# Forming the first attention scores earlier, and adding the last block's attention in halves from an earlier tile, in a fused attention and mixture-of-experts kernel

## The chip, the cores and the metric

The kernel runs on one core of a Trainium2 chip. The metric is the device time of one execution in microseconds (us), lower is better; the number quoted is the median of several runs. A core has five engines that run side by side and wait for each other through semaphores: PE (TensorE, matrix multiplies and transposes), DVE (VectorE), ACT (ScalarE), POOL (GpSimd, which here mostly issues gathers and adding stores) and SP (SyncE, which here only issues DMA).

## What is computed

The input is x of shape (8, 1024, 256). Its rows are layer-normalised, then two results are added to x: causal linear attention of 16 heads, and a mixture of 8 experts of which each row uses two. Cut to what matters:

```python
xn = layernorm(x)
q = elu(xn @ Wq.T) + 1; k = elu(xn @ Wk.T) + 1; v = xn @ Wv.T      # 16 heads of 16
kv_cumsum = cumsum(k_outer_v, axis=1); k_cumsum = cumsum(k, axis=1)
att = (q . kv_cumsum) / clip(q . k_cumsum, 1e-6) @ Wo.T
w, e = top_k(xn @ Wr + br, 2); w = softmax(w)
moe = sum over both e of w_e * (silu(xn @ W1[e]) * (xn @ W3[e])) @ W2[e]
out = x + att + moe
```

All data are float32.

## The kernel before, in words

The 8192 rows form 16 blocks of 512 (two per sequence). The experts' work is not done by blocks but by tiles: rows that chose the same expert are listed, and tiles of 128 listed rows are gathered from x in device memory, multiplied with that expert's weights and added back to the output by an indirect store. There are 135 tiles, of which the last three run only if they hold rows, so the main loop has NM = 132 tiles.

*The start* (lines 1047 to 1118) is written in a fixed order for DVE, ACT, PE and POOL. The first four blocks are normalised, turned and routed (`moments`, `normalise`, `turn`, `logits`, `route`), and `first_batch` makes from them the list of the first 25 tiles. Beside it block 0's q, k and v are projected. At its end stand the row statistics of block 5 (`moments(FB + 1, 1)`, DVE), three steps of block 0's attention (`attend_upto(3, False)`: transposes of k, L858, and on DVE the running sums of k, L863 to L868), two matmuls whose result nobody reads (`idle_ps`, L1113), and a switch of ACT to the Silu table (L1118). Meanwhile POOL gathers the rows of tile 0 (`ffn_load`, L1162 the rows, L1167 their weights and norm numbers).

*The main loop* (line 1285) does for tile j: `ffn_step` (load tile j + 3, weights of tile j + 2 through SP, the hidden products gu_ps L1216, the turning of tile j + 1's rows xg_t L1183, the output y_ps L1235 of tile j - 1, and its adding store L1246 on POOL). In the first tiles it also normalises, turns and routes the remaining blocks, and it calls `attend_upto`, which advances the attention. Outside the part with a fixed order a scheduler places the instructions on each engine.

*The attention* is a generator of 9 steps per block, 144 in all (`block_steps`, line 995). Steps 1 to 4 project q, k, v and form the denominators (den, L880; over, L886; they go through device memory by den_d and return as rden, L892 and L898); step 5 forms the scores of the block's first 128 rows (`scores`: s_ps, L919, in four banks of the pool ps_mm; the mask s_sb on DVE, L926; the state kv_ps L934 and kv L939); steps 6 to 9 weigh (`weigh`: o_ps, L953 and L960, oT) and multiply with Wo (`attend`: a_ps L979, ACT's copy into at L984). A block's four quarters of at are added to the output by one POOL DMA at its end (L989); only the last block adds each quarter by itself (L987). How far the attention is at tile j comes from a formula in the loop: slow up to tile 21, and from tile 22 on evenly (L1325), so that the last step runs at tile 127.

*What orders writes of the output.* Adding DMAs to the same array wait for the one before to land, and POOL issues them one after another.

Of the kernel before, what the change touches and what calls it, by code (L numbers as in the profile page):

```python
# [53 lines left out]
P = 128  # L54
# [9 lines left out]
def tile_attention_moe(  # L64
# [208 lines left out]
    def moments(t, n):  # L273


        def small(name, *shape, dtype=F32):
            return f_two.tile([P, n * NCH, *shape], dtype, tag=name, name=name)

        less, rstd = (tab[:, t * NCH : (t + n) * NCH, w] for w in (1, 2))
        st = small("st", 6)  # L280
        mv = small("mv", 2)
        for c in range(n * NCH):
            nc.vector.bn_stats(st[:, c, :], xbs[t + c // NCH][:, c % NCH, :])
            nc.vector.bn_aggr(mv[:, c, :], st[:, c, :])
        v = small("v")
        nc.vector.tensor_scalar(v, mv[:, :, 1], EPS_NORM, None, ALU.add)
        if t <= FB:
            nc.gpsimd.tensor_tensor(rstd, v, neg_half, ALU.pow)
        else:

            half = small("half")
            nc.vector.tensor_scalar(half, v, -0.5, None, ALU.mult)
            bits = small("bits", dtype=I32)
            nc.vector.tensor_scalar(bits, v.bitcast(I32), 1, None, ALU.arith_shift_right)
            nc.vector.tensor_scalar(bits, bits, -1.0, float(0x5F3759DF), ALU.mult, ALU.add)
            y = bits.bitcast(F32)
            for i in range(4):
                sq = small("sq")
                nc.vector.tensor_tensor(sq, y, y, ALU.mult)
                nc.vector.tensor_tensor(sq, sq, half, ALU.mult)  # L300
                y_new = small(f"y{i % 2}") if i < 3 else rstd
                nc.vector.scalar_tensor_tensor(y_new, sq, 1.5, y, ALU.add, ALU.mult)
                y = y_new
        yield
        nc.vector.scalar_tensor_tensor(less, mv[:, :, 0], -1.0, rstd, ALU.mult, ALU.mult)
        yield
# [665 lines left out]
    def attend(t, c, oT):  # L972


        if c == 0:
            ats[t] = one.tile([P, NCH, H], F32, tag="at", name=f"at{t}")
        a_ps = ps_y.tile([P, H], F32, tag="y", name="a_ps")
        for hh in range(2):
            nc.tensor.matmul(  # L979
                a_ps, lhsT=oT[:, hh, :], rhs=wo_sb[:, hh, :],  # L980
                start=(hh == 0), stop=(hh == 1),
            )
        at = ats[t]
        nc.scalar.copy(at[:, c, :], a_ps)  # L984
        to = acc_f if t < FB and not copied else of
        if t == NBLK - 1:
            nc.gpsimd.dma_start(out=to[t][:, c, :], in_=at[:, c, :], accum_op=ALU.add)  # L987
        elif c == NCH - 1:
            nc.gpsimd.dma_start(out=to[t], in_=at, accum_op=ALU.add)  # L989
        if c == NCH - 1:  # L990
            del ats[t], blocks[t]
# [3 lines left out]
    def block_steps(t):  # L995


        for i, _ in enumerate(project(t)):
            if i == 1 and behind:
                attend(*behind.pop())  # L1000
            if i in (1, 3, 5, 8):
                yield
        if t + 1 < NBLK:
            fetch(t + 1)
        waiting = scores(t, 0)
        yield
        done = None
        for c in range(NCH):
            coming = scores(t, c + 1) if c + 1 < NCH else None
            if done and c + 1 < NCH:  # L1010
                attend(*done)
            oT = weigh(*waiting)
            if done and c + 1 == NCH:
                attend(*done)
            done = t, c, oT
            waiting = coming
            if c + 1 < NCH or t + 1 < NBLK:
                yield
        behind.append(done)
        if t + 1 == NBLK:  # L1020
            attend(*behind.pop())
            yield
# [24 lines left out]
    with tc.manual_schedule(engines={EN.DVE, EN.Activation, EN.PE, EN.Pool}):  # L1047
        parts = [moments(t, 1) for t in range(FB)]
        lgT4 = e_one.tile([P, FB, P], F32, name="lgT4")
        small_constants()  # L1050
        next(parts[0])
        qs = [project_q(0, o) for o in range(KC)]
        for t in range(FB):
            if t + 1 < FB:
                next(parts[t + 1])
            next(parts[t])
            normalise(t)
            turn(t)
            if t == 1:
                logits(0, lgT4[:, 0, :])  # L1060
            elif t == 0:
                xnTs[0] = turned_first.pop()
                begin(0)
            if t < KC:
                next(qs[t])
        last_moments = moments(FB, 1)
        next(last_moments)
        for t in range(1, FB):
            logits(t, lgT4[:, t, :])
        for _ in last_moments:  # L1070
            pass
        lg4 = ps_t.tile([P, FB * P], F32, tag="t", name="lg4")
        for t in range(FB):
            nc.tensor.transpose(lg4[:, bass.ts(t, P)], lgT4[:, t, :], ident)
        store(FB - 1)
        add_logits(0, FB, lg4)
        for q in qs:
            next(q)
        normalise(FB)
        ks = [project_k(0, c) for c in range(0, NCH, 2)]  # L1080
        routing = route(0, FB)
        next(routing)
        next(ks[0])
        next(routing)
        turn(FB)
        next(ks[1])
        for q in qs:
            next(q)
        next(routing)
        listing = first_batch()  # L1090
        next(listing)
        next(routing)
        lg_t = logits_turned(FB)
        vs = [project_v(0, c) for c in range(0, NCH, 2)]
        next(vs[0])
        next(listing)
        next(vs[0])
        next(listing)
        add_logits(FB, 1, lg_t)
        next(listing)  # L1100
        for o in range(KC):
            mask_q(0, o)
        next(vs[1])
        for k in ks:
            next(k)
        for _ in moments(FB + 1, 1):
            pass
        next(vs[1])
        attend_upto(3, False)

        for _ in range(2):
            idle_ps = ps_mm.tile([P, TB], F32, tag="mm", name="idle_ps")
            nc.tensor.matmul(  # L1113
                idle_ps, lhsT=ident, rhs=blocks[0][0][:, 0, :], start=True, stop=True
            )
        next(routing)

        nc.scalar.activation(warm, ones[:, 0:1], AF.Silu)  # L1118
# [166 lines left out]
    for j in range(NM + 1):  # L1285
        if j + 1 < NM:
            ffn_norm(j + 1)
        t = FB + j
        if FB < t <= NBLK and t % ROUND == 0:
            for _ in routing:  # L1290
                pass
        if 0 < j and t < NBLK:
            if j % 2 == 0:
                with tc.issue_after(last_token[0].ins):
                    for _ in moments(t, 2):
                        pass
            normalise(t)
            turn(t)
            if t + 5 < NBLK:
                load_x(t + 5, nc.scalar)  # L1300
            add_logits(t, 1, logits_turned(t))
            if (t + 1) % ROUND == 0:
                routing = route(t + 1 - ROUND, t + 1)
                next(routing)
        if j == LISTS:
            in_order(
                nc.sync.dma_start(
                    out=tab_d[1][1 : 1 + NS * P, :].rearrange("(p i) w -> p (i w)", p=P),
                    in_=tab.rearrange("p i w -> p (i w)"),
                )  # L1310
            )
            in_order(nc.sync.dma_start(out=tab_d[1][0:1, :], in_=before[0:1, 0:3]))
            lists = second_batch(taken)
        if LISTS <= j < READ:
            next(lists)
        if LISTS <= j < LISTS + NBLK - FB:
            t = FB + j - LISTS
            rows = slice(t * TB, (t + 1) * TB)
            in_order(nc.sync.dma_start(out=out_rows[rows, :], in_=x_rows[rows, :]))
        if j < LISTS:  # L1320
            attend_upto(3 + j // 2)
        elif j < READ:
            attend_upto(AHEAD - 3 * (READ - j - 1) // 2)
        else:
            attend_upto(AHEAD + (NBLK * STEPS - AHEAD) * (j - READ + 1) // (NM - READ - 4))  # L1325
        if j == N1 + 1:
            copied.append(j)
            in_order(nc.sync.dma_start(out=out_rows[0 : FT * P, :], in_=acc_d[:, :]))
        ffn_step(j, LATE if N1 < j <= N1 + LATE else 0)
# [54 lines left out]
```

## Time and profile before

| | us |
|---|---|
| median of 3 runs | 1318.28 (1317.63 to 1319.15) |
| the profiled execution's own time | 1329.68 |
| its span, first to last instruction | 1328.0 |
| PE busy in the span | 1270.6 |
| DVE, ACT, POOL busy | 636.9, 526.1, 523.1 |
| last matmul of the gu_ps group ends | 1314.6 |

The profile is of one execution. A busy share is an average over stages; what a stage is bound by is read from the stretch itself: which engine is full there, and which wait ends last. In a timeline line the first number is the start in us from the span's start, the second the duration, and the bracket gives the idle time of that engine just before and what ended it. A matmul of float32 leaves two records, so "x32" are 16 matmuls. "PEclk" is the share of the full clock that PE was granted.

### The profile page before, as it was taken

To read this page: it belongs to the slowest core of one execution; us is meant where nothing else is said; L and a number is where in the kernel's file an instruction comes from. 1 tells how busy PE (TensorE), PEld (TensorE's weight loads), DVE (VectorE), ACT (ScalarE), POOL (GpSimd) and SP (SyncE) were. 2 spreads that over 40 slices of the span, in tenths; PEclk is the share of its full clock that TensorE was granted. 3 is DMA by queue.
4 is the path that set the end of the run, shared out by engine and by line. 5 is a ranking of instruction groups with operands and counts; after the bars stand their busy time and mean duration, and the time that the engine had idled before them with its cause. 6 is when DMAs were issued, how large, how long until landed. Compare 5 with 4: busy or idle time off the path is not lost.

```text
span 1328.0 us, 28290 instructions
## 1 busy us (share of the span) xinstructions
PE 1270.6 (96%) x10968; PEld 1092.2 (82%) x10968; DVE 636.9 (48%) x1436; ACT 526.1 (40%) x1060; POOL 523.1 (39%) x460
## 2 busy tenths in 40 slices
PE   5689999999999999999999999999999999999996
PEld 4478887787888888888888888898888888888886
DVE  7667489764252434435343535344443525243441
ACT  4466364461524325161525243341515152433411
POOL 3633333233254443443443525343434334343432
PEclk9899999999999999999999999999999999999998
DMA  9688576466685766666675757476676767575763
GB/s 340 229 276 258 154 200 170 130 173 206 176 229 141 198 166 155 189 173 172 169 190 145 216 132 208 126 188 171 160 186 170 189 153 194 147 198 134 198 161 72
DMA packets 163462, 240.36 MB, mean 181 GB/s; under 512 B 16098, under 2 KB 87394, under 8 KB 163042
## 3 DMA queue, kind: packets, MB, share of 16 engines
q1 hardware_dynamic: 119938, 184.31, 45.0%
q0 software_dynamic: 38064, 43.22, 19.3%
q10 hardware_dynamic: 5328, 11.01, 2.3%
q8 instruction: 90, 1.47, 0.5%
q14 instruction: 42, 0.34, 0.1%
HBM read 196.30 MB, written 52.67 MB: 187 GB/s over the span
## 4 chain that ended last, share of the span: by engine, by line
PE 87%; DVE 7%; ACT 2%; issue 1%; DMA 1%; another core or an unknown queue 1%; POOL 0%; POOLq 0%; DVEq 0%; ACTq 0%
PE gu_ps L1216 34%; PE y_ps L1235 16%; PE o_ps L960 5%; PE s_ps L919 5%; PE a_ps L979 4%; PE zq L795 4%; PE zkk L811 4%; PE zkv L811 4%; PE kv_ps L934 2%; PE o_ps L953 2%; PE xg_t L1183 2%; DVE s_sb L926 1%; PE tp L333 1%; PE den L880 1%; PE tp L858 1%
## 5 line engine op out<-in xcount | busy, mean ns | idle before, releaser
L1216 PE MATMUL gu_ps<-xgT,w 128*128 128x128 f32 x4224 | 511.2, 278 | 8.9 <-DVE s_sb L926 7.6
L1216 PEld LDWEIGHTS gu_ps<-xgT,w 128*128 128x128 f32 x4224 | 492.5, 193 | 28.8 <-issue 12.5
L1162 POOL DMA_INDIRECT xg<-in_x_dram,src_i x132 | 128.1, 970 | 406.1 <-ACT xgT L1185 322.4
L1246 POOL DMA_INDIRECT out_dram<-y,dst_i x107 | 176.3, 1648 | 222.2 <-DVE kn L765 54.2
L1235 PE MATMUL y_ps<-w_sb,hT 128*128 x1056 | 250.6, 380 | 2.6 <-DVE hT L1227 2.0
L1227 DVE TENSOR_TENSOR hT<-gu_ps,hT 128x512 f32<-128x512 f32 x132 | 91.1, 690 | 274.4 <-PE gu_ps L1216 198.0
L1235 PEld LDWEIGHTS y_ps<-w_sb,hT 128*128 128x128 f32 x1056 | 190.2, 190 | 24.0 <-DVE hT L1227 1.9
L1224 ACT ACTIVATE hT<-gu_ps 128x512 f32<-128x512 f32 x132 | 78.8, 597 | 299.9 <-PE gu_ps L1216 255.0
L926 DVE TENSOR_TENSOR s_sb<-s_ps,causal 128x512 f32<-128x512 f32 x256 | 163.6, 684 | 54.0 <-PE s_ps L919 25.5
L1242 DVE TENSOR_SCALAR y<-y_ps,entry 128x256 f32<-128x256 f32 x132 | 63.5, 481 | 120.0 <-PE y_ps L1235 75.0
L1167 POOL DMA_INDIRECT entry<-tab_d,of_i x107 | 106.5, 995 | 32.6 <-issue 30.5
L1185 ACT COPY xgT<-xg_t 128x256 f32<-128x256 f32 x132 | 49.0, 371 | 145.2 <-PE xg_t L1183 141.7
L984 ACT COPY at<-a_ps 128x256 f32<-128x256 f32 x64 | 23.7, 370 | 159.2 <-PE a_ps L979 149.0
L919 PE MATMUL s_ps<-qm,kT 32*128 32x256 f32 x1024 | 85.5, 405 | 0.5 <-DVE hT L1227 0.4
L1174 ACT ACTIVATE xg<-xg,entry 128x256 f32<-128x256 f32 x132 | 79.6, 603 | 3.4 <-issue 3.4
L960 PE MATMUL o_ps<-s_sb,va 128*32 128x128 f32 x2048 | 73.2, 276 | 0.0
L919 PEld LDWEIGHTS s_ps<-qm,kT 32*128 32x128 f32 x1024 | 51.0, 184 | 24.2 <-issue 19.6
L979 PE MATMUL a_ps<-wo_sb,oT 128*128 128x256 f32 x256 | 69.0, 393 | 0.1
L1246 POOL DMA_INDIRECT acc_d<-y,src_i x25 | 44.0, 1761 | 55.2 <-DVE y L1242 15.4
L960 PEld LDWEIGHTS o_ps<-s_sb,va 128*32 128x32 f32 x2048 | 53.2, 109 | 9.8 <-DVE oT L967 0.8
L811 PE MATMUL zkk<-wkv_sb,xnT 128*128 128x256 f32 x256 | 60.0, 384 | 0.0
L795 PE MATMUL zq<-xnT,wq_sb 128*128 128x512 f32 x128 | 59.9, 609 | 0.0
(211 smaller groups left out, 1361.7 us busy)
## 6 DMA issues: line engine op xcount, KB each, us to landing
w<-in_w_dram SPq DMA_DIRECT2D x264, 512.0 KB
den_d<-over SPq DMA_DIRECT2D x64, 128.0 KB
rden<-den_d SPq DMA_DIRECT2D x16, 512.0 KB
xnT_d<-xnT ACTq DMA_DIRECT2D x15, 512.0 KB
xnT<-xnT_d SPq DMA_DIRECT2D x15, 512.0 KB
out_dram<-in_x_dram SPq DMA_DIRECT2D x12, 512.0 KB
out_dram<-at POOLq DMA_DIRECT2D x12, 512.0 KB
xb<-in_x_dram SPq DMA_DIRECT2D x10, 512.0 KB
```

What stands on the lines that cost most here:

```text
L795: nc.tensor.matmul(z, lhsT=wq_sb[:, k, bass.ts(o, P)], rhs=xnTs[t][:, k, :], start=(k == 0), stop=(k == KC - 1),)
L811: nc.tensor.matmul(z[:, i, :], lhsT=xnTs[t][:, k, bass.ts(c + i, P)], rhs=wkv_sb[:, k, a, :], start=(k == 0), stop=(k == KC - 1),)
L919: nc.tensor.matmul(s_ps[r][:, hh].rearrange("p a l -> p (a l)"), lhsT=kT[rows, hh, span], rhs=qm[rows, hh, :, span], start=True, stop=True,)
L926: nc.vector.tensor_tensor(sm, s_ps[r].rearrange("p k a l -> p (k a) l"), causal_b, ALU.mult)
L960: nc.tensor.matmul(o_ps[32 * r : 32 * r + 32, hh, :], lhsT=va[:, c, 4 * hh + r, a, :], rhs=s_sb[r][:, 2 * hh + a, :], start=(first and a = ...
L979: nc.tensor.matmul(a_ps, lhsT=oT[:, hh, :], rhs=wo_sb[:, hh, :], start=(hh == 0), stop=(hh == 1),)
L1162: nc.gpsimd.indirect_dma_start(out=xg[j], out_offset=None, in_=x_rows[:, :], in_offset=bass.IndirectOffsetOnAxis(ap=src_i[:, i : i + 1], a ...
L1167: nc.gpsimd.indirect_dma_start(out=entry[j], out_offset=None, in_=table[:, :], in_offset=bass.IndirectOffsetOnAxis(ap=num_i[:, i : i + 1], ...
L1216: done = nc.tensor.matmul(ps[:, i, :], lhsT=w13[:, k, bass.ts(i, P)], rhs=xgT[j][:, k, :], start=(k == 0), stop=(k == KC - 1),)
L1227: nc.vector.tensor_tensor(hT, gu[1], hT, ALU.mult)
L1235: done = nc.tensor.matmul(y_ps, lhsT=hT[:, i, :], rhs=w2_sb[:, bass.ds(e * (IC * H) + i * H, H)], start=(i == 0), stop=(i == IC - 1),)
L1246: nc.gpsimd.indirect_dma_start(out=rows[:, :], out_offset=bass.IndirectOffsetOnAxis(ap=dst_i[:, i : i + 1], axis=0), in_=ys.pop(j), in_off ...
```

## The change

Four edits:

- In block 0's attention the scores of the first 128 rows are formed after step 3, before the denominators (`if t == 0 and i == 5`); for other blocks nothing moves. Step 4 and step 5 of block 0 change places.
- In the start, `attend_upto(3, False)` is followed by `attend_upto(4)`, so those scores belong to the fixed order, and both stand ahead of the statistics of block 5. The idle matmuls are four in place of two and use one buffer of the pool ps_y, since the scores hold all four banks of ps_mm.
- The last block adds its attention in two halves of 256 columns by 128 rows by two, in place of four quarters.
- The formula of L1325 ends three tiles earlier (NM - READ - 7 in place of NM - READ - 4): the last attention step runs at tile 124.

```diff
         if t == NBLK - 1:
-            nc.gpsimd.dma_start(out=to[t][:, c, :], in_=at[:, c, :], accum_op=ALU.add)
+            if c % 2 == 1:
+                two_c = slice(c - 1, c + 1)
+                nc.gpsimd.dma_start(
+                    out=to[t][:, two_c, :], in_=at[:, two_c, :], accum_op=ALU.add
+                )
         elif c == NCH - 1:
...
             if i in (1, 3, 5, 8):
                 yield
+            if t == 0 and i == 5:
+                waiting = scores(t, 0)
+                yield
         if t + 1 < NBLK:
             fetch(t + 1)
-        waiting = scores(t, 0)
-        yield
+        if t > 0:
+            waiting = scores(t, 0)
+            yield
...
         for k in ks:
             next(k)
+        next(vs[1])
+        attend_upto(3, False)
+        attend_upto(4)
         for _ in moments(FB + 1, 1):
             pass
-        next(vs[1])
-        attend_upto(3, False)
-
-        for _ in range(2):
-            idle_ps = ps_mm.tile([P, TB], F32, tag="mm", name="idle_ps")
+
+        idle_ps = ps_y.tile([P, TB], F32, tag="y", name="idle_ps")
+        for _ in range(4):
             nc.tensor.matmul(
                 idle_ps, lhsT=ident, rhs=blocks[0][0][:, 0, :], start=True, stop=True
             )
...
-            attend_upto(AHEAD + (NBLK * STEPS - AHEAD) * (j - READ + 1) // (NM - READ - 4))
+            attend_upto(AHEAD + (NBLK * STEPS - AHEAD) * (j - READ + 1) // (NM - READ - 7))
```

## The prediction

> **What bounds the kernel now.** I read the page first: the busy shares and the chain that ended last.
>
> ```profile
> PE 1270.6 (96%) x10968; PEld 1092.2 (82%) x10968; DVE 636.9 (48%) x1436; ACT 526.1 (40%) x1060; POOL 523.1 (39%) x460
> ```
> ```profile
> PE 87%; DVE 7%; ACT 2%; issue 1%; DMA 1%; another core or an unknown queue 1%; POOL 0%; POOLq 0%; DVEq 0%; ACTq 0%
> ```
>
> TensorE (PE) is the bound, so an edit pays only where PE stands still. The view by stretches says where: from 400 to 1300 us PE is busy 99.5%; it is idle in the first 100 us and after the last matmul at 1314.6 us. The columns are PE, PEld, DVE, ACT and POOL busy us, granted clock, DMA share, GB/s:
>
> ```profile
> 40.00:50.00 10.00, 6.88 (x78) 4.42 (x70) 7.77 (x38) 5.82 (x12) 5.06 (x5) 1.00 1.02 344
> 50.00:60.00 10.00, 6.51 (x36) 5.88 (x36) 5.55 (x29) 1.47 (x3) 7.63 (x8) 0.66 0.27 76
> 60.00:70.00 10.00, 6.49 (x47) 5.66 (x48) 6.63 (x39) 5.16 (x11) 1.42 (x2) 0.83 0.43 138
> 90.00:100.00 10.00, 6.77 (x55) 5.37 (x54) 7.67 (x30) 5.61 (x9) 2.60 (x2) 1.00 1.07 321
> ```
>
> The timeline of PE, ACT and DVE then names the waits (start, duration, in brackets the idle time before and its releaser):
>
> ```profile
> 45.84 1.88 PE L1113 MATMUL idle_ps<-qT,ident 128*128 128x512 f32 x4
> 52.21 0.69 PE L1183 MATMUL xg_t<-ident,xg 128*128 128x128 f32 x2 [4.49 <-issue]
> 53.36 5.61 PE L1216 MATMUL gu_ps<-xgT,w 128*128 128x128 f32 x32 [0.46 <-issue]
> 63.49 0.33 PE L333 MATMUL tp<-ident,xb 128*128 128x128 f32 x1 [4.31 <-ACT xb L318]
> 91.67 1.15 PE L919 MATMUL s_ps<-qm,kT 32*128 32x256 f32 x16
> 96.22 2.27 PE L1216 MATMUL gu_ps<-xgT,w 128*128 128x128 f32 x18 [2.76 <-DVE s_sb L926]
> 98.97 0.49 PE L443 MATMUL cnt_ps<-both,upto_neg 128*128 128x128 f32 x2 [0.47 <-DVE both L429]
> ```
> ```profile
> 62.36 0.60 ACT L1224 ACTIVATE hT<-gu_ps 128x512 f32<-128x512 f32 x1 [8.55 <-remote]
> ```
>
> PE is idle 4.5 us while tile 0's rows come; then tile 0 runs 5.61 us where 32 such records take 3.57 us later (chain, 1292.69); PE waits 4.3 us for ACT, which had itself waited 8.55 us for something the trace does not show (gu_ps was finished by 58.97); and tile 0's scores, formed inside the PE-bound stretch, hold PE 2.76 us because DVE masks them late. At the end POOL's row-adding stores follow each other:
>
> ```profile
> 1293.50 1.61 POOL L1246 DMA_INDIRECT out_dram<-y,dst_i  x1 [4.51 <-DVE y L1242]
> 1299.96 1.56 POOL L1246 DMA_INDIRECT out_dram<-y,dst_i  x1 [4.85 <-DMA out_dram<-y,dst_i]
> 1306.28 1.55 POOL L1246 DMA_INDIRECT out_dram<-y,dst_i  x1 [4.76 <-DMA out_dram<-y,dst_i]
> 1310.82 1.55 POOL L1246 DMA_INDIRECT out_dram<-y,dst_i  x1 [3.00 <-issue]
> 1316.18 1.55 POOL L1246 DMA_INDIRECT out_dram<-y,dst_i  x1 [3.81 <-DVE hT L1227]
> 1320.84 1.55 POOL L1246 DMA_INDIRECT out_dram<-y,dst_i  x1 [3.11 <-DMA out_dram<-y,dst_i]
> ```
>
> The last y is ready at 1317.91 (DVE L1242), its store starts 2.93 us later, because the store ahead of it had not landed.
>
> **What the Trainium skill says.** "TensorE: Matmul & The Clock Gate", section "What's actually happening": after an idle window of about 3.4 us PE's clock falls to half, and about 3.4 us of work brings it back. The trace agrees: idle 47.72 to 52.21, clock 0.50 from 51 to 57 us. "DMA: Bandwidth & Descriptors", section "Two DMAs through the same engine are not ordered": a DMA that touches bytes of an earlier one must wait for its completion semaphore. The trace agrees: three of the six stores above were released by the previous store's DMA. Same page, section "Anatomy of one DMA — SWDGE (gpsimd) path": about 2.0 us fixed plus bytes/436e3, so as an estimate a 256 KB half costs 2.6 us and two 128 KB quarters 4.6 us one after the other; the trace has 4.2 to 5.3 us between POOL's last-block entries, neighbours included. Same page, "Issuing engines are not separate DMA queues": all share 16 engines; the stores above are 6.46 and 6.32 us apart while weights load (last issue 1300.03) and 4.54 to 5.36 after.
>
> **The change, part by part.** All sums stand against the profiled execution, 1329.68 us with a span of 1328.0; that is 11.4 us above the median 1318.28. The unexplained 8.55 us gap cost PE 4.3 us plus about 1.6 us of half clock (64 to 67.3), so it may be part of that excess. I work the start both without the gap (N) and with it (G).
>
> *Scores into the gather.* Removed from the stretch at 91.67: 8 s_ps and 2 kv_ps matmuls (1.7 us of PE, to 93.46), four s_sb and one kv on DVE (4 x 0.60 + 0.36). They now stand behind the k transposes: kT is ready at 46.68, so PE has them done near 48.4, inside the 4.5 us gap, cost nothing. Four idle matmuls at 0.94 (1.88 for two) then fill to 52.2, when xg_t can start; the clock should stay full and tile 0's gu takes 3.6 in place of 5.6. They use a ps_y buffer; if they overran, at most 0.5 us.
>
> *Statistics of block 5 moved behind the scores on DVE.* In the built order DVE now does, from 45.07 on: wait for kT to 46.2, two scans (1.20), two multiplies (0.6), four s_sb, kv: to about 52.8. Only then the statistics, which before took 45.0 to 54.2; with hT(0) (0.6) standing among them, tab is ready near 62.7. ACT's normalise (4 x 0.6), and PE's transposes of that block, queue behind it; PE has finished tiles 0 and 1's gu by 61.2 and waits. Behind those transposes stand the logits, xg_t(2), lg_t and y(0). Following ACT's order (normalise to 65.2, one more normalise at 66.1 that waits for the next statistics, two xnT copies to 67.7, two DMA issues 0.9, lgT) y(0) starts near 69.6.
> Before, in N: tab at 54.3, tp at 59, gu(1) beside it, y(0) near 66.0. So +3.6. In G: before 72.0; after, gu(1) starts at 63.4 behind the same gap, y(0) near 72.6: +0.6. Half clock after a thin stretch 61 to 69: 0 to 1.6, I take 0.8.
>
> *den moves two tiles later.* Its 8 matmuls (0.6), over (0.29 + 0.94), four den_d DMAs and rden pass two tiles of weight loads in SP's queue. From over to rden's issue it was 11.7 us (81.99 to 93.69); two tiles give some 20, so I take 0; up to 2 if oT waits for rden on DVE, with hT behind it. The fetch of xnT moves with it and is not wanted before tile 12.
>
> *Tile 4.* gu(4) no longer waits behind s_sb. Its counts (cnt_ps) still wait for DVE's routing, which starts after the xb DMA issued at 84.46 lands at 92.15. Without the 2.4 us of s_sb, "both" comes 4.3 us after that landing in place of 6.75; PE has by then done all 32 gu records, 14 more (1.55 us). Gain about 4.0 after paying den's 0.6; 2 to 5.5, as the xb DMA may land sooner without den_d beside it; I take 4.4.
>
> Start, N: 3.6 + 0.8 - 4.4 = 0.0. G: 0.6 - 4.4 = -3.8.
>
> *Middle.* 121 attention steps spread over 103 tiles, not 106: the same PE work, so 0; stalls by DVE there total some 14 us and move about, +-1.5.
>
> *End.* Last attend at tile 124 in place of 127; nothing on PE saved. POOL saves two issues of 0.9, hidden. But nine stores, not six, now follow each other at y's pace of 5.52 us (1292.73 to 1298.25), while a store under weight loads takes 6.3 to 6.5. The lag grew 0.29, 1.23, 2.03 in the old tail; three more tiles may add up to 0.85 each, less what the last quiet tiles give back. Bounds 0 and 3.0 (the lag can't shrink: the first of the six was on time); I take 1.2, since at a lag the store falls into other gaps of the weight traffic (one pair in mid-kernel was 5.52 apart).
>
> Sum N: 0.0 + 0 + 1.2: 1319.5 on the median.
>
> **Rivals.** *Faster:* the gap is real in every run, or ACT's queue is not held by the statistics; then the full clock, the avoided 2.76 and the 1.7 count. For it: the gap is in the trace. Against: 11.4 us of excess want an explanation. -3.8 and up to -1.6 for the second half-clock stretch, +1.2: 1314.3. *Slower:* the late statistics. Place: PE's first tp of block 5; price 3.6 plus 1.6 of half clock, with tile 4 giving back only 2; it decides as soon as PE is through gu(1) (61.2) before tab (62.7). With the tail at 2.5: 1324. For it: DVE is 1.00 busy from 45 to 53, so the pushed work has no slack. Against: ACT and DVE orders may let PE use that time. *Tail only:* start nets nothing and lag grows in full: 1321.3. That scores don't move is excluded: the built order shows them ahead of the idle matmuls.
>
> **How the numbers follow.** Forecast N 0.42 (its own range 1316.5 to 1322.5), faster 0.25, slower 0.25, tail only 0.08. A measurement of this kernel tells about 0.2% from no change, 2.6 us: bounds 1315.6 and 1320.9. From N one sixth lies above and little below; so faster 0.26, same 0.38, slower 0.36. Range 1313.5 to 1324.5.
>
> **What would show it.** Clock 1.0 and gu(0) near 3.6 us in 50 to 60; a PE wait at tp L333 near 61 to 65 with tab late (right for N and the slower rival; absent for the faster one); no wait at s_sb near 90; last store's start minus last y over 2.93 us. I am wrong if PE does not wait for block 5, or if the middle's stalls change by more than 2 us.

## The result, and the profile after

The changed kernel took 1323.23 us (median of 7 runs, 1322.84 to 1326.34) where the kernel before took 1319.84 (7 runs, 1317.63 to 1321.21). The ratio is 1.0034 with a 95% interval of 1.0022 to 1.0045: slower by a third of a per cent (the ratio weighs all runs; the medians alone lie 3.4 us apart). The profiled execution of the changed kernel has a span of 1321.2 us and an own time of 1323.23, so unlike the profile of before it is a typical one.

The page of the changed kernel, busy shares and chain:

```profile
PE 1273.1 (96%) x10972; PEld 1091.4 (83%) x10972; DVE 636.0 (48%) x1436; ACT 526.4 (40%) x1060; POOL 524.5 (40%) x458
PE 87%; DVE 8%; ACT 2%; DMA 2%; issue 1%; POOL 0%; POOLq 0%; ACTq 0%; DVEq 0%
```

The shares hardly differ from those before: a loss of 0.3% lies in a few waits. The stretches of the changed kernel (us, then busy us of PE, PEld, DVE, ACT, POOL, granted clock, DMA share, GB/s) show where the start was altered:

```profile
50.00:60.00 10.00, 8.53 (x61) 6.75 (x60) 10.00 (x47) 3.18 (x7) 7.56 (x9) 1.00 0.48 143
60.00:70.00 10.00, 6.66 (x44) 4.07 (x42) 8.05 (x58) 5.44 (x12) 3.17 (x4) 0.72 0.68 213
```

From 50 to 60 us PE is busy 8.53 us at full clock (6.51 at 0.66 before), and DVE is full. From 60 to 70 PE stands still as long as before and its clock has dropped. Below, gu(j) and y(j) are the hidden products and the output of tile j, and tab holds the scale and shift with which a block's rows are normalised. The timelines of PE and of ACT in the changed kernel name the waits:

```profile
48.17 3.60 PE L1122 MATMUL idle_ps<-qT,ident 128*128 128x512 f32 x8
...
53.22 3.84 PE L1225 MATMUL gu_ps<-xgT,w 128*128 128x128 f32 x32 [0.46 <-ACT xgT L1194]
...
63.82 0.33 PE L333 MATMUL tp<-ident,xb 128*128 128x128 f32 x1 [2.69 <-ACT xb L318]
...
70.46 3.75 PE L1244 MATMUL y_ps<-w_sb,hT 128*128 x8 [0.55 <-DVE lg_all L367]
...
116.32 1.16 PE L1225 MATMUL gu_ps<-xgT,w 128*128 128x128 f32 x8 [2.23 <-DVE s_sb L926]
```
```profile
63.17 2.08 ACT L318 ACTIVATE xb<-xb,tab 128x256 f32<-128x256 f32 x4 [2.74 <-DVE tab L305]
```

Tile 0's gu takes 3.84 us (5.61 before). Then PE waits 2.69 us for the normalised rows of block 5, for which ACT has waited for tab. y(0) runs at half clock. The wait of a gu for s_sb, 2.76 us at 96 us before, is gone from there, and one of 2.23 us stands at 116 us. ACT's gap of 8.55 us is not in this profile. The last stores on POOL:

```profile
1304.35 1.55 POOL L1255 DMA_INDIRECT out_dram<-y,dst_i  x1 [2.94 <-issue]
1309.62 1.55 POOL L1255 DMA_INDIRECT out_dram<-y,dst_i  x1 [3.72 <-issue]
1314.18 1.55 POOL L1255 DMA_INDIRECT out_dram<-y,dst_i  x1 [3.00 <-DMA out_dram<-y,dst_i]
```

The last y is ready at 1310.62, so its store starts 3.56 us later; before it was 2.93 us.

### The profile page after: what moved, and what is told of

Its sections match the earlier page's. It is cut to its first block, busy times and chain, and to the rows that moved or that the text cites. A ratio compares the mean times of both kernels' runs of the same rounds, so it can differ in the third digit from the quotient of the medians.

```text
span 1321.2 us, 28291 instructions
## 1 busy us (share of the span) xinstructions
PE 1273.1 (96%) x10972; PEld 1091.4 (83%) x10972; DVE 636.0 (48%) x1436; ACT 526.4 (40%) x1060; POOL 524.5 (40%) x458
## 4 chain that ended last, share of the span: by engine, by line
PE 87%; DVE 8%; ACT 2%; DMA 2%; issue 1%; POOL 0%; POOLq 0%; ACTq 0%; DVEq 0%
PE gu_ps L1225 34%; PE y_ps L1244 16%; PE s_ps L919 5%; PE o_ps L960 5%; PE a_ps L979 4%; PE zq L795 4%; PE zkk L811 4%; PE zkv L811 4%; PE kv_ps L934 2%; PE xg_t L1192 2%; PE o_ps L953 2%; DMA xb<-in_x_dram 1%; DVE st L283 1%; PE tp L858 1%; PE tp L333 1%
```

## The experiments

Each was timed beside the kernel before, in three comparisons on three chips. There the kernel before took 1327.4 to 1328.7 us, 8 to 9 us more than in the first comparison, whose chip is not on record. Whether the chip or the gap on ACT makes that difference was not separated. Ratios are to the kernel before of the same comparison.

**The kernel before once more, and the changed kernel once more** (no edit).

> The kernel before, unchanged, profiled a second time. Its first profile had a span of 1328.0 us, 8 us over its timed median, with a gap of 8.55 us on ACT in the start that nothing in the trace explains. If the gap was of that one execution, the new profile shows a span near 1317, no such gap, y(0) near 66 and the ratio is 1.000. If the gap belongs to the kernel, it is there again, y(0) is near 72, and the start of the changed kernel (y(0) at 70.5) gained instead of lost.

> The changed kernel, unchanged, beside the kernel before in the same call. If the start (1.0025 alone) and the end (1.0015 alone) simply add, the ratio is 1.004 (1.003 to 1.005). Its own first profile had no stall on ACT before 63 us; in the last call all four kernels had one, in which the semaphore of PE told of matmuls of 54 to 59 us only at 62.7. If that stall belongs to the program, it is here again and y(0) is near 78; if it depends on the chip, y(0) follows what before shows on the same chip.

Measured: 1.0000 (0.9991 to 1.0008) and 1.0032 (1.0017 to 1.0046), profiled spans 1326.2 and 1328.8. ACT's gap is in both. ACT in the kernel before, profiled again, and then in the changed kernel:

```profile
62.75 0.60 ACT L1224 ACTIVATE hT<-gu_ps 128x512 f32<-128x512 f32 x1 [8.37 <-remote]
```
```profile
63.02 0.37 ACT L1194 COPY xgT<-xg_t 128x256 f32<-128x256 f32 x1 [6.70 <-remote]
```

In both, ACT goes on at about 63 us with an instruction that waits for PE, which had ended that work 5.0 us earlier (the first of the two gu_ps of tile 0, all that this instruction reads, at 57.72) and 6.5 us earlier (xg_t, at 56.48). So 5.0 of the 8.37 us are a hold-up and the rest is PE's own work. The name "remote" says that the profile finds no instruction near the update of the semaphore. The gap belongs to neither kernel alone, and the loss is the same third of a per cent here (1.0032) as in the first comparison (1.0034), where the profile of the changed kernel had no gap. Of the two outcomes that were named for the kernel before, the second came: the gap again, and y(0) at 72.35. For the changed kernel the ratio lay in its range, but y(0) came at 73.89 and not near 78.

**The start alone**: the changed kernel with the old end.

```diff
-            if c % 2 == 1:
-                two_c = slice(c - 1, c + 1)
-                nc.gpsimd.dma_start(
-                    out=to[t][:, two_c, :], in_=at[:, two_c, :], accum_op=ALU.add
-                )
+            nc.gpsimd.dma_start(out=to[t][:, c, :], in_=at[:, c, :], accum_op=ALU.add)
...
-            attend_upto(AHEAD + (NBLK * STEPS - AHEAD) * (j - READ + 1) // (NM - READ - 7))
+            attend_upto(AHEAD + (NBLK * STEPS - AHEAD) * (j - READ + 1) // (NM - READ - 4))
```

> The changed kernel's start (scores of block 0 ahead of the statistics of block 5, idle matmuls in another bank), with the four quarter additions and the pace of the kernel before. Theory of the late statistics: y(0) stays near 70.5, all of the loss is here, ratio near 1.003. Theory of the end (longer queue of additions and stores): the loss was in the tail, ratio 0.999 to 1.000. Theory of the middle (attention paced to end three tiles earlier): the same, 0.999 to 1.000.

**The end alone**, and its two halves: the kernel before with the new pace and the two halves (tail_only), with the two halves (halves_only), with the pace (pace_only). The diffs are the two pieces above, turned round.

> The start of the kernel before, with the last block's attention added in two halves and paced to end three tiles earlier. Theory of the late statistics: ratio 1.000 (0.999 to 1.001), the last store starts 0.6 us later after its y than in the kernel before. Theory of the end: ratio 1.003, with the last lag of y to store 4 us longer. Theory of the middle: ratio 1.003, with the loss spread over the y times of tiles 28 to 120.

> The kernel before with two halves in place of four quarters, the pace as before (attention ends at tile 127). It parts the 0.15% of the end. If the two larger additions cost it: 1.0015. If the earlier end (three tiles earlier, so that nine stores stand one behind the other and the attention of the middle comes sooner) costs it: 1.000 (0.9995 to 1.0005), since two additions fewer stand among the last stores.

> The kernel before with the attention paced to end three tiles earlier, and still four quarters. The end as a whole gave 1.0015 and the halves alone 1.0005. If the pace costs the rest: 1.001 (1.000 to 1.002). If the two act only together: 1.0000 (0.9995 to 1.0005).

| | ratio | 95% interval | us of 1328 |
|---|---|---|---|
| start alone | 1.0025 | 1.0015 to 1.0035 | 3.3 |
| end alone | 1.0015 | 1.0004 to 1.0026 | 2.0 |
| halves alone | 1.0005 | 0.9997 to 1.0014 | 0.7 |
| pace alone | 1.0013 | 1.0002 to 1.0025 | 1.7 |

Start and end add up to 1.0040, the whole is 1.0032 to 1.0034: within their intervals they are additive. Both lose; no theory that puts all in one place holds. Of the end the pace seems the larger part, though the two intervals overlap, and the halves can't be told from no change.

**The statistics of block 5 ahead of other work on DVE.** In the first trace of the changed kernel sixteen statistics of later blocks (0.4 us each) stand ahead of block 5's tab on DVE, eleven of them between the steps that follow block 5's own four. stats_alone holds them behind block 5's last step (those of blocks 6 and 7, and with them all later ones); both_late also puts block 0's running sums (L863 to L868) behind it.

```diff
+    last_stat = [None]
...
-        nc.vector.scalar_tensor_tensor(less, mv[:, :, 0], -1.0, rstd, ALU.mult, ALU.mult)
+        last_stat[0] = nc.vector.scalar_tensor_tensor(
+            less, mv[:, :, 0], -1.0, rstd, ALU.mult, ALU.mult
+        )
...
-                with tc.issue_after(last_token[0].ins):
+                with tc.issue_after((last_stat if j == 2 else last_token)[0].ins):
```

Only in both_late, where `sum_up` holds the scan, the copy and the multiply:

```diff
-            qks.append(ksum)
+            if t > 0:
+                qks.append(sum_up(o))
...
+        if t == 0:
+            with tc.issue_after(last_stat[0].ins):
+                for o in range(KC):
+                    qks.append(sum_up(o))
```

> The changed kernel with the statistics of blocks 6 and 7 held behind the last step of block 5's: eleven of their operations (0.42 us each) no longer stand between block 5's steps. Theory of the late statistics: tab of block 5 comes about 3 us earlier than in the changed kernel of the same call, y(0) 2 to 3 us earlier, ratio to before 1.002 against 1.004. Theory of the stall (ACT is held until about 62.7 whatever DVE has done) or of a wait that only moves to a later block's scores: tab comes earlier, but the end doesn't, ratio 1.004.

> The changed kernel with block 0's running sums (two scans and two multiplies, 3.7 us of DVE) put behind the statistics of block 5, and the statistics of blocks 6 and 7 kept behind those of block 5 (in the changed kernel 11 of them stand between its steps). Theory of the late statistics: tab of block 5 is written near 56.5 instead of 63.0, PE has no wait of 2.7 us at the transposes of block 5, y(0) comes near 66, and the run is 3 to 4 us faster than the changed kernel: ratio 1.000 (0.999 to 1.001) to the kernel before. Theories of the end and of the middle: nothing in this part of the start sets the end, ratio stays 1.003.

stats_alone gave 1.0005 (0.9997 to 1.0014), 0.27% better than the changed kernel in the same comparison (2.8 us between the medians). tab came at 58.20 in place of 65.94. But the profile doesn't show the gain reach the end. Against after_again, y(0) starts 1.8 us earlier on PE (72.10 against 73.89) and y(5) 2.2 us earlier, but y(8) 0.4 us later: between y(5) and y(6) PE waits 2.79 us for oT, which is the first to use the denominators. That execution (1330.71) was one of its slower ones. both_late gave 1.0045 (1.0034 to 1.0056), a miss: tab came at 56.17, as expected, but ACT was held in the gap until 62.76 all the same, and the later sums made the denominators late. PE in both_late:

```profile
131.96 0.66 PE L337 MATMUL tp<-ident,xb 128*128 128x128 f32 x4 [4.26 <-DVE oT L980]
```

Here PE waits 4.26 us for oT. The changed kernel has no such wait, but all three runs that bring tab forward have one: 2.79 us in stats_alone, 4.26 here, 3.60 in stats_five below.

**The queue of gathers on POOL.** Up to the first hidden layer POOL issues 13 gathers one after another, eight of them the entries of tiles 0 to 7, for which there are eight buffers. before_five has five buffers, before_four four; after_five is the changed kernel with five, stats_five is stats_alone with five.

```diff
-        entry[j] = ffn8.tile([P, 3], F32, tag="entry", name="entry")
+        entry[j] = ffn5.tile([P, 3], F32, tag="entry", name="entry")
```

> The kernel before with five buffers for the gathered entries instead of eight, so that POOL issues 10 gathers up to the first hidden layer instead of 13, and the entries of tiles 5 to 7 come after the first stores. If the queue of gathers on POOL is what holds back the semaphores in the stall, the stall ends with POOL's queue, some 3.7 us earlier (near 59 instead of 62.7), and the run is up to 3.7 us faster: ratio 0.997 to 0.998. If not, the stall ends near 62.7 again and the ratio is 1.000 (0.999 to 1.001).

> The kernel before with four buffers for the gathered entries: 9 gathers up to the first hidden layer instead of 13 (before) or 10 (before_five). If the stall ends about 2 us after POOL's last gather of the queue, it ends near 56 or is gone, as gu(0)'s first half is through at 55: ratio 0.995 (0.994 to 0.996). If before_five gained for another reason, such as another order of gathers later on, no further gain: 0.996 or above, the more as the entry of tile 4 now waits for the first y.

> The changed kernel with five buffers for the gathered entries, as before_five is of the kernel before (0.9958). With the shorter queue of gathers the stall of ACT should end near 58. If the stall alone hid what the earlier scores gain, this is as fast as before_five: 0.995 to 0.997. Theory of the late statistics (block 5's tab stands behind the scores and between the statistics of blocks 6 and 7 whatever the gathers do) and of the score wait that only moves to tile 5: the distance to before_five stays that of the changed kernel to before, 0.3 to 0.5%: ratio 0.999 to 1.001.

> after_five with the statistics of blocks 6 and 7 held behind block 5's. Theory of the late statistics: faster than after_five by about what stats_alone gained on the changed kernel, 0.2 to 0.3%; tab of block 5 near 58, no wait of over 1 us at the first transposes of block 5. If stats_alone's gain came by way of the stall instead, this is equal to after_five.

| | gathers in the queue | last ends, us | PE's work done, us | ACT goes on, us | ratio | 95% interval |
|---|---|---|---|---|---|---|
| before_again | 13 | 60.70 | 57.72 | 62.75 | 1.0000 | 0.9991 to 1.0008 |
| after_again | 13 | 60.99 | 56.48 | 63.02 | 1.0032 | 1.0017 to 1.0046 |
| before_five | 10 | 55.45 | 55.86 | 57.39 | 0.9958 | 0.9946 to 0.9971 |
| before_four | 9 | 56.33 | 57.70 | 57.73, not held | 1.0050 | 1.0033 to 1.0067 |
| after_five | 10 | 57.87 | 57.61 | 59.40 | 1.0000 | 0.9987 to 1.0012 |
| stats_five | 10 | 57.17 | 54.40 | 58.03, waits for tab | 1.0000 | 0.9989 to 1.0010 |

"PE's work done" is the end of the work for which ACT's waiting instruction needs PE: gu_ps of tile 0 or xg_t of tile 1. In stats_five ACT stood waiting for tab, so a hold-up can't be told there.

POOL and ACT in before_five, the last gather of the queue and ACT's first instruction after the gap:

```profile
54.50 0.95 POOL L1162 DMA_INDIRECT xg<-in_x_dram,src_i  x1 [0.30 <-issue]
```
```profile
57.39 0.60 ACT L1224 ACTIVATE hT<-gu_ps 128x512 f32<-128x512 f32 x1 [4.31 <-remote]
```

With three gathers fewer the queue ends 5.25 us earlier, the gap ends 5.36 us earlier, y(0) starts 6.6 us earlier (65.71), and the kernel before becomes 0.42% faster: it beats both kernels. ACT is held for 5.0 us after PE's work with 13 gathers, 1.5 with 10 and not at all with 9. So in the kernel before, by one profile each, the number of gathers in the queue decides how long ACT is held. Whether the queue itself does it, or the transfers that belong to it, these runs don't separate. With four buffers the hold-up is gone, but the run is slower than before: at 96.64 us a gu waits 7.51 us for s_sb. With five buffers the changed kernel stays 0.42% behind (1.0000 against 0.9958, on two chips), as the theory of the start's own loss wanted: the gap did not hide a gain of the earlier scores. The order of the statistics gave nothing clear of noise there (1.0000 both; tab at 57.83 in place of 62.84), so the 0.27% of stats_alone is not confirmed by the second pair.

## Why the prediction was right and wrong

The forecast was 1319.5 with a range of 1313.5 to 1324.5; it is 1323.23. The time lies in the range, but the likeliest case, no change, was not what happened: 1.2 us of loss were forecast, 3.4 measured. The rival "late statistics" with 1324 came nearest. Its parts, 3.2 us in the start and 2.5 at the end, are even close to the 3.3 and 2.0 of the experiments, but that is partly luck: it gave tile 4 less than it gained, knew nothing of the loss behind tile 4, and put the end's loss into the stores, where little of it is.

**Scores into the gather: right on PE, worth less than it looks.** Clock 1.00 and gu(0) at 3.84 us were forecast as 1.0 and 3.6. But where ACT has the gap, both kernels go on at 63 us whatever PE had done by then.

**Late statistics: right without the gap.** tab at 62.99 (forecast 62.7), the PE wait at the transposes of block 5, y(0) at 70.46 (forecast 69.6, and half clock, 3.75 us for y(0) in place of 1.97). Where the gap is in both kernels, y(0) was forecast 0.6 us later and is 1.5 us later (73.89 against 72.35), in the start-alone run 2.6 (74.96). There PE does not wait at the transposes of block 5, which I had named as a sign of being wrong: it waits 6.96 and 7.02 us at gu(1), for ACT in its gap. tab is later still (65.94 and 65.66), and in after_again DVE itself twice waits 0.83 us between block 5's steps, so what makes the gap may have a part in that. How much of the late statistics reaches the end stays open, as said: one pair of experiments gave 0.27%, the other nothing.

**den later: 0 only in part.** In the changed kernel PE has no wait for oT. But the wait is there as soon as tab comes earlier (2.79 and 3.60 us), and 4.26 when the sums go later still. And the transfers that moved with den stand where the loss behind tile 4 arises (next part).

**Tile 4: the step that failed.** I wrote "Gain about 4.0 after paying den's 0.6; 2 to 5.5 ... I take 4.4". Start of y on PE, as distance to before_again, all from the timelines:

| us | y(0) | y(1) | y(2) | y(3) | y(4) | y(5) | y(8) |
|---|---|---|---|---|---|---|---|
| after_again | +1.54 | +0.64 | -0.72 | -3.20 | -0.77 | +1.28 | +1.63 |
| start_only | +2.61 | +1.72 | +0.35 | -3.18 | -1.76 | +0.26 | +0.62 |

From y(0) to y(3) the change gains 4.7 and 5.8 us, so the wait at tile 4 was rightly seen and the sum about right; but only 2.5 and 3.5 us of it lie between y(2) and y(3), where I had put 4.4. From y(3) to y(5) it loses 4.5 and 3.4, and at y(8) nothing of it is left in after_again and 2.0 us in start_only: I stopped adding too early. PE in the kernel before, in its second profile, then DVE at the same place:

```profile
96.51 2.27 PE L1216 MATMUL gu_ps<-xgT,w 128*128 128x128 f32 x18 [2.68 <-DVE s_sb L926]
...
113.41 0.70 PE L919 MATMUL s_ps<-qm,kT 32*128 32x256 f32 x4
...
114.62 1.13 PE L919 MATMUL s_ps<-qm,kT 32*128 32x256 f32 x12
```
```profile
112.63 0.75 DVE L283 BATCH_NORM_STATS2 st<-xb 128x6 f32<-128x256 f32 x2 [0.16 <-DMA xb<-in_x_dram]
...
115.38 1.89 DVE L926 TENSOR_TENSOR s_sb<-s_ps,causal 128x512 f32<-128x512 f32 x3 [0.60 <-PE s_ps L919]
```

The changed kernel in its second profile, the timelines of PE and DVE and one stretch:

```profile
107.60 0.71 PE L919 MATMUL s_ps<-qm,kT 32*128 32x256 f32 x6
109.38 0.69 PE L919 MATMUL s_ps<-qm,kT 32*128 32x256 f32 x2 [1.07 <-issue]
110.17 3.11 PE L1244 MATMUL y_ps<-w_sb,hT 128*128 x8
...
114.33 0.69 PE L919 MATMUL s_ps<-qm,kT 32*128 32x256 f32 x2
...
115.31 0.69 PE L919 MATMUL s_ps<-qm,kT 32*128 32x256 f32 x2
...
116.28 0.70 PE L919 MATMUL s_ps<-qm,kT 32*128 32x256 f32 x4
...
119.08 1.16 PE L1225 MATMUL gu_ps<-xgT,w 128*128 128x128 f32 x8 [0.45 <-DVE s_sb L926]
```
```profile
116.45 0.75 DVE L283 BATCH_NORM_STATS2 st<-xb 128x6 f32<-128x256 f32 x2 [5.89 <-DMA xb<-in_x_dram]
...
118.36 1.27 DVE L926 TENSOR_TENSOR s_sb<-s_ps,causal 128x512 f32<-128x512 f32 x2
```
```profile
110.00:114.00 4.00, 4.00 (x15) 3.28 (x15) 0.19 (x1) 0.58 (x2) 0.00 (x0) 0.58 1.04 365
```

The next step's 16 score records, which came in two pieces (1.83 us), come in five (3.48): 1.65 lost. Before one of them PE waits 1.07. y(4) takes 3.11 at a clock of 0.58 in place of 1.89: 1.22. A gu waits 0.45 for s_sb. Together 4.4 of the 4.5 us; the account is rough, since the records of neighbours overlap a little and the transposes behind y(4) are slow too (1.32 us for six, 0.82 before). In the first profile of the changed kernel and in start_only the same place shows four pieces and a wait of 2.23 and 2.00 us for s_sb instead of the slow y(4). So the wait for masked scores had not been removed, it stands one step on.

What makes the masks late there is not a full DVE. DVE stands idle for 5.89 us (6.60 in the first profile, 6.13 in start_only) for the rows of a later block, whose statistics (L283) are ahead of the masks in its order; in the kernel before the same statistics wait 0.16. ACT issues the load of those rows at 104.85 (107.00 in the kernel before), and DVE can start on them 11.6 us later in place of 5.6; the neighbouring loads in the two traces took 5.4 to 9.5. Beside it now run the transfers that moved with den: four den_d from 101.10 on and the fetch of xnT at 105.54, which in the kernel before were issued from 83.88 on and at 90.51. That these slow the load fits the timing but is not shown, since no run moved them alone. In the kernel before, too, the masks at 96 us had been late behind such statistics (2.10 us of waiting for rows at 92.17 in its first trace). Why the scores come in pieces, I did not test. Where the forecast's start was 0.0 without and -3.8 us with the gap, the start alone measures +3.3 (2.0 to 4.6); the profiles show 0.6 and 1.6 of it at y(8), their executions being among the faster ones of their kernels.

**Middle: 0 forecast, within +-1.5.** The pace alone costs 1.7 us (0.3 to 3.3). In its profile, of one of its slower executions, 1.0 us more than in before_again lies between y(28) and the last y, and the last store's lag is 3.98 in place of 2.92. Which waits make up that 1.0 was not followed.

**End: the lag was mis-sized.** Forecast +1.2; the last store starts 0.63 later after its y in the first pair of profiles, 0.49 in the second, 0.29 in tail_only. The bound of 0 held, but the lag was priced to grow from store to store, and it doesn't. In the changed kernel it reaches 3.99 us at the third of the nine stores and is back at 1.87 at the seventh, since stores 4.49 to 5.44 us apart catch up with a y every 5.52; I had priced them at 6.3 to 6.5. With the last two y, which come closer together, it is 3.63 and 3.56. (The end is also not where I had put it: 1314.6 is the last gu, and PE's last matmul, of y, ends at 1317.39.)

**The gap.** I had taken the 11.4 us of excess of the first profile as a reason to doubt it. It was there in the later profiles of both kernels, and the rival "faster", which rested on it, lost anyway.

## What to carry to other kernels

A wait that is taken away on the bounding engine counts only where the distance between the two traces stays constant; follow it tile by tile until it does, because the next step can meet what made the first one late. And look at what the late engine was doing: DVE's masks were late while DVE stood idle, behind an instruction that waited for a transfer. A gap for which a profile names no releaser deserves a second profile and a look at what other queue ends just before the gap does: here five buffers in place of eight moved the time more than the whole change did. Work that is brought forward on one engine (PE's scores) is paid for on an engine that is full at that time (DVE, from 50 to 60 us), so cost what it pushes back, transfers included.

## What the runs showed of the hardware

In the profiles that have the gap, the trace's records of PE's semaphore (the one that ACT waits for) carry no update between 55.70 and 62.95 us in after_again, and then two within 0.1 us, though PE had ended the work before 57; DVE's own semaphore advances about every 0.7 us (57.12, 57.83, 58.54, 59.26, 59.96) while its small instructions take 0.15 to 0.42. In the eleven profiles in which ACT is held, it goes on 1.5 to 2.6 us after the last gather of POOL's queue ends. The first profile of the changed kernel had as long a queue, until 63.00, and no gap; so the queue alone doesn't make it, and what does is open.

The clock fell to 0.58 from 110 to 114 us after a stretch (107 to 110) in which PE was busy 1.93 of 3 us and never idle for longer than 1.07. The Trainium skill, "TensorE: Matmul & The Clock Gate", section "What's actually happening", names an idle window of about 3.4 us as what drops it; here the clock fell without one, after a thin stretch.
